# Last batch of a four-layer graph network: adj's transpose and layers 2 and 3 in buffers of layer 0, layer 3 by halves, and a new set of order constants

## The chip, the cores and the metric

The kernel runs on one core of one Trainium2 chip. The metric is the device time of one execution in microseconds (us), the median of the runs shown. Engines are named as in the profile: PE is TensorE (matmul), PEld its weight loads, DVE is VectorE, ACT is ScalarE, POOL is GpSimd, SP is SyncE, which here only issues DMAs.

## The reference

32 graphs ("batches") of 512 nodes with 128 features each, and a 0/1 adjacency matrix per graph with about 16 ones per row. Four layers follow one another, each on the normalised and rectified nodes, each added to `x`:

```
h = relu(layernorm(x)); x = x + max_j( relu(p_i + q_j + b) * adj[i, j] )          # layer 0
h = relu(layernorm(x)); x = x + four tanh layers of: (adj/|row|) @ (f ws), f wn,
                            (adj/|col|).T @ (f wd), each with wu                     # layer 1
h = relu(layernorm(x)); x = x + (adj / rowsum) @ (h w) + bias                       # layer 2
h = relu(layernorm(x)); 4 times:                                                    # layer 3
    m = adj.T @ (h weight[l])
    r, z = sigmoid(m w_ih + h w_hh + b);  n = tanh(m w_ih_n + b_n + r * (h w_hh_n + c_n))
    h = (1 - z) * n + z * h
x = x + h * mask
```

The batches don't depend on each other. Within one batch everything from layer 1 on is one chain: sublayer after sublayer.

## The kernel before, in words

Nodes lie in four tiles of 128 (`NT = 4`), so a batch's node features are one 128 x 512 tile. `an` is the adjacency matrix of a batch in SBUF, `at` its transpose, made on PE and moved out by ACT. Layer 0 (functions `prepare` and `gathers`) finds each node's largest neighbours in two ways at once: 28 indirect DMAs per batch on POOL's queue gather rows of a table (`G`, `gm`, with DVE maxima), and for the rest one-hot matrices (`oh`, made on DVE from `ccd`) pick rows by matmul into `pa`, with DVE maxima into `acc`. Layer 1 is `layer1`, layers 2 and 3 are `layer23`. A float32 operand of an aggregation is split in a high and a low part (`hi`, `lo`), so an aggregation is eight matmuls `pg`.

In layer 3, one sublayer goes: transposes `ph` of the new `h` (PE), `hi` (ACT), `lo` (DVE), aggregation `pg` (PE), `mT` (ACT), the two gates `pk` (PE: a part with `h`, early, and a part with `mT`), two sigmoids (ACT), `phn` and `pxn` (PE), `nn` (DVE twice, then tanh on ACT), then `z*h` on POOL and the new `h` by two DVE instructions. Each handles the whole 128 x 512 tile.

The order of every engine's instructions is fixed when the program is built. A small list scheduler (class `Flow`) holds the operations of up to `AHEAD = 6` batches, keeps a model clock for every engine, and gives out next what can start first; of those that can start at the same time it takes the one with the earliest due time. The due time is `place * PACE - (longest way to the batch's end) - lead`: `place` is the batch's number moved by `LAST`, the lead comes from the table `LEADS`, by stage. A larger lead therefore means: earlier in the queue. `WEIGHTS` are the places of three pieces of weight preparation that are ordered the same way. Where PE would be idle by the model for over 1 us, matmuls without use (`spin`) are put in, so that the granted clock stays up.

Buffers set the rest of the order. A tag (`hi2`, `mT`, `at`, ...) is a ring of so many buffers, handed out strictly in the order of the batches; an operation that writes a buffer for the first time waits until the tile that held it has been read for the last time. Layers 2 and 3 own one buffer each of `xn2`, `hi2`, `lo2`, `mT`, `hg` (the state `h`), `gate0`, `gate1`, `zc`, `nn`; layer 1 has its own ones. `at` and `an` have three each, `af` (the adjacency matrix as loaded) one, `ccd` six. The eight PSUM banks are shared: the four groups `ps0` (layer 0's preparation), `ps1` (layer 1), `ps2` (layers 2 and 3) and `ps3` (layer 0's `pa`) keep 2, 1, 2 and 1, and two are lent to whoever asks.

Of the kernel before, what the change touches and what calls it, by code (L numbers as in the profile page):

```python
# [13 lines left out]
F32 = mybir.dt.float32  # L14
F32R = mybir.dt.float32r
# [3 lines left out]
AF = mybir.ActivationFunctionType  # L19
ALU = mybir.AluOpType  # L20
# [4 lines left out]
P = 128  # L25
# [6 lines left out]
KEY = float(ROWS)  # L32
CODES = ((0, 1), (P, 1), (2 * P, 2), (4 * P, 4))
NLEFT = 7
PACE = 45.28
SPACING = 1.8
AHEAD = 6
BANKS = (2, 1, 2, 1)

LEADS = {  # L40
    "prepare": -31.3, "counts": -26.1, "keys": -29.9, "rows": -0.7,
    "gather0": 21.0, "gather1": 4.8, "gather2": 6.6, "gather3": -2.7,
    "first": 14.9, "layer1": -15.8, "layer10": -31.7, "layer11": -34.7,
    "layer12": -17.6, "layer13": -49.5, "layer2": 17.3, "layer3": 7.8,
    "layer30": 58.6, "layer31": 78.0, "layer32": 36.2, "layer33": 30.6,
    "out": 18.1,
}
LAST = (0.0, 0.0, -0.31, -0.67, 0.62)
WEIGHTS = (-4.52, -3.22, -3.0)
LN_EPS = 1e-5  # L50
L2_EPS = 1e-12
LOWEST = float(np.finfo(np.float32).min)
# [7 lines left out]
def flat(t):  # L60
    return t.rearrange("p t d -> p (t d)")
# [755 lines left out]
def fast(ctx: ExitStack, tc: tile.TileContext, a: dict, out: bass.AP, bad):  # L817
    nc = tc.nc
    x, adj, nodemask = a["x"], a["adj"], a["nodemask"]
    B, N, D = x.shape  # L820
    assert D == P and N % P == 0
    NT = N // P
# [6 lines left out]
    F = Flow(nc, PACE, AHEAD)  # L829
# [5 lines left out]
    def pst(s, name):  # L835
        return bank(s, [P, NT, P], F32, name)

    big = ctx.enter_context(tc.tile_pool(name="big", bufs=1))
    mid = ctx.enter_context(tc.tile_pool(name="mid", bufs=1))
    W = FastWeights(nc, F, a, const, mid, ps)  # L840
# [6 lines left out]
    for i in range(2):  # L847
        t = dram.tile([ROWS, P], F32, name=f"qtab{i}")
        k = (ROWS - 2 * P) // P
        nc.sync.dma_start(  # L850
            out=t[2 * P :, :].rearrange("(k p) d -> p k d", p=P),
# [10 lines left out]
        F.act.dma_start(out=af, in_=adj[b].rearrange("(t p) j -> p t j", p=P))  # L862
        return xt, af

    def norm(s, xt, tag):

        st = F.tile(small, [P, NT, nc.vector.BN_STATS_DIM], F32, tag=f"st{s}", name=f"st_{tag}", bufs=4)
        mv = F.tile(small, [P, NT, nc.vector.BN_AGGR_DIM], F32, tag=f"mv{s}", name=f"mv_{tag}", bufs=4)
        for t in range(NT):
            F.vec.bn_stats(st[:, t, :], xt[:, t, :])  # L870
        for t in range(NT):
            F.vec.bn_aggr(mv[:, t, :], st[:, t, :])
        rstd = F.tile(small, [P, NT], F32, tag=f"rstd{s}", name=f"rstd_{tag}", bufs=4)
        F.vec.tensor_scalar(rstd, mv[:, :, 1], LN_EPS, None, ALU.add)
        F.pool.tensor_tensor(rstd, rstd, W.mhalf[:, 0:NT], ALU.pow)
        shift = F.tile(small, [P, NT], F32, tag=f"shift{s}", name=f"shift_{tag}", bufs=4)
        F.vec.tensor_scalar(shift, mv[:, :, 0], -1.0, None, ALU.mult)
        F.pool.tensor_mul(shift, shift, rstd)
        xn = F.tile(mid, [P, NT, P], F32, tag=f"xn{s}", name=f"xn_{tag}")
        for t in range(NT):  # L880
            F.act.activation(
                xn[:, t, :], xt[:, t, :], AF.Relu,
                bias=shift[:, t : t + 1], scale=rstd[:, t : t + 1],
            )
        return xn

    def transposed(s, src, name):

        pt = pst(s, name)
        for t in range(NT):  # L890
            F.tr(pt[:, t, :], src[:, t, :], W.ident)
        return pt

    def sbuf_parts(s, src, tag):

        hi = F.tile(mid, [P, NT, P], F32R, tag=f"hi{s}", name=f"hi_{tag}")
        F.act.copy(hi, src)
        lo = F.tile(mid, [P, NT, P], F32R, tag=f"lo{s}", name=f"lo_{tag}")
        F.pool.tensor_sub(lo, src, hi.bitcast(F32))
        return hi, lo  # L900

    def parts(s, src, tag):

        hi = F.tile(mid, [P, NT, P], F32R, tag=f"hi{s}", name=f"hi_{tag}")
        F.act.copy(hi, src)
        lo = F.tile(mid, [P, NT, P], F32R, tag=f"lo{s}", name=f"lo_{tag}")
        F.vec.tensor_sub(lo, src, hi.bitcast(F32))
        return hi, lo

    def aggregate(s, two, m, name):  # L910

        pg = pst(s, name)
        hi, lo = two
        for jt in range(NT):
            F.mm(flat(pg), hi[:, jt, :], m[:, jt, :], start=(jt == 0), stop=False)
            F.mm(flat(pg), lo[:, jt, :], m[:, jt, :], start=False, stop=(jt == NT - 1))
        return pg


    def prepare(b, xt, af):  # L920

        deg = F.tile(small, [P, 2, NT], F32, tag="deg", name=f"deg_{b}", bufs=4)
        xn = norm(0, xt, f"{b}_0")
# [10 lines left out]
        pt = transposed(0, xn, f"pt_{b}_0")  # L934
        hT = F.tile(mid, [P, NT, P], F32, tag="hT0", name=f"hT_{b}_0")
        F.act.copy(hT, pt)
        at = F.tile(big, [P, NT, N], F32R, tag="at", name=f"at_{b}", bufs=3)
        for half in range(NT // 2):
            pt = bank(0, [P, 2, N], BF16, f"pat_{b}_{half}")
            for u in range(2):  # L940
                jt = 2 * half + u
# [9 lines left out]
        qn = F.tile(mid, [P, NT, P], F32, tag="qn", name=f"qn_{b}")  # L951
# [34 lines left out]
        ccd = []  # L986
# [161 lines left out]


    def layer23(b, x2, an, at, dinv):  # L1150
        xn = norm(2, x2, f"{b}_2")
        two = sbuf_parts(2, xn, f"{b}_2")
        F.pool.tensor_add(x2, x2, W.b2.unsqueeze(1).to_broadcast([P, NT, P]))
        pg = aggregate(2, two, at, f"pg2_{b}")
        mT = F.tile(mid, [P, NT, P], F32, tag="mT", name=f"mT2_{b}")
        F.act.copy(mT, pg)
        po = pst(2, f"po_{b}")
        for t in range(NT):
            F.mm(po[:, t, :], mT[:, t, :], W.w2, start=True, stop=True)
        x3 = x2  # L1160
        F.lead = LEADS["layer3"]
        for t in range(NT):
            F.vec.scalar_tensor_tensor(
                x3[:, t, :], po[:, t, :], dinv[:, t : t + 1], x2[:, t, :], ALU.mult, ALU.add
            )
        xn = norm(2, x3, f"{b}_3")
        two = sbuf_parts(2, xn, f"{b}_3")
        pt = transposed(2, xn, f"pt_{b}_3")
        h = F.tile(mid, [P, NT, P], F32, tag="hg", name=f"h_{b}_3")
        F.act.copy(h, pt)  # L1170
        for l in range(W.NL3):
            F.lead = LEADS[f"layer3{l}"]
            gates = []
            for k in range(2):
                pk = pst(2, f"pk_{b}_{l}_{k}")
                F.mm(flat(pk), W.gh[l][:, k, :], flat(h), start=True, stop=False)
                gates.append(pk)
            pg = aggregate(2, two, an, f"pg3_{b}_{l}")
            mT = F.tile(mid, [P, N], F32, tag="mT", name=f"mT_{b}_{l}")
            F.act.copy(mT, flat(pg))  # L1180
            for k in range(2):
                F.mm(flat(gates[k]), W.gm[l][:, k, :], mT, start=False, stop=True)
                g = F.tile(mid, [P, N], F32, tag=f"gate{k}", name=f"gate{k}_{b}_{l}")
                c = 3 * l + k
                F.act.activation(g, flat(gates[k]), AF.Sigmoid, bias=W.bsum[:, c : c + 1])
                if k == 1:

                    zc = F.tile(mid, [P, N], F32, tag="zc", name=f"zc_{b}_{l}")
                    F.pool.tensor_scalar(zc, g, -1.0, 1.0, ALU.mult, ALU.add)
                gates[k] = g  # L1190
            r, z = gates
            c = 3 * l + 2
            phn = pst(2, f"phn_{b}_{l}")
            F.mm(flat(phn), W.gh[l][:, 2, :], flat(h), start=True, stop=True)
            nn = F.tile(mid, [P, N], F32, tag="nn", name=f"nn_{b}_{l}")
            F.vec.scalar_tensor_tensor(
                nn, flat(phn), W.bhh[:, c : c + 1], r, ALU.add, ALU.mult
            )
            pxn = pst(2, f"pxn_{b}_{l}")
            F.mm(flat(pxn), W.gm[l][:, 2, :], mT, start=True, stop=True)  # L1200
            F.vec.tensor_add(nn, flat(pxn), nn)
            F.act.activation(nn, nn, AF.Tanh, bias=W.bih[:, c : c + 1])

            F.pool.tensor_mul(z, flat(h), z)
            hn = F.tile(mid, [P, NT, P], F32, tag="hg", name=f"h_{b}_{l}")
            F.vec.tensor_mul(nn, nn, zc)
            F.vec.tensor_add(flat(hn), z, nn)
            h = hn
            pt = transposed(2, h, f"ph_{b}_{l}")
            if l + 1 < W.NL3:  # L1210
                two = parts(2, pt, f"{b}_3_{l}")
        F.lead = LEADS["out"]
        xo = F.tile(mid, [P, NT, D], F32, tag="mT", name=f"xo_{b}")
        for t in range(NT):
            c = b * NT + t
            F.vec.scalar_tensor_tensor(
                xo[:, t, :], pt[:, t, :], W.mcol[:, c : c + 1], x3[:, t, :], ALU.mult, ALU.add
            )
        F.act.dma_start(out=out[b].rearrange("(t p) d -> p t d", p=P), in_=xo)
# [15 lines left out]

    F.spin = spin

    places = [b - LAST[max(0, b - B + len(LAST) - 1)] for b in range(B)]
    F.run(
        list(zip(WEIGHTS, (W.first, W.rest, W.last)))  # L1240
        + [(p, partial(batch, b)) for b, p in enumerate(places)]
# [471 lines left out]
```

## Time and profile before

| | |
|---|---|
| median of 3 runs | 2977.16 us (2974.79 to 2977.79) |
| the profiled execution, device time | 2976.68 us |
| its span, first to last instruction | 2975.0 us |
| PE busy | 2861.7 us, of which 69.7 us are `spin` |
| DVE, POOL, ACT busy | 2393.3, 1819.8, 1216.1 us |
| PE clock granted | 0.990 of full speed on average |
| one batch in the middle of the run | 87 us |

The profile comes from one execution, and the times in it are microseconds from the first instruction. All compute instructions are issued from a few helper lines, so groups are told apart by the names of their tiles (out<-in), not by lines. A busy PE isn't a PE at work on the result: the `spin` matmuls count as busy.

### The profile page before, as it was taken

Reading aid. Unit: us, or ns where it says so; the run is one execution under the profiler, and the core shown is the slowest. Engines: PE = TensorE matmul, PEld = TensorE weight load, DVE = VectorE, ACT = ScalarE, POOL = GpSimd, SP = SyncE. Lnnn points to the kernel's source line nnn. Section 1 sums busy time; section 2 is a strip of 40 time slices with the busy share of each in tenths; the row PEclk is TensorE's granted clock in tenths of the full one; section 3 lists DMA queues with packets and bytes.
Section 4 is the critical chain, followed back from the end, with each engine's and each line's share of the span. In section 5 each row is a group of like instructions: output and inputs, shape, how many; then the busy total and the mean of one; then the engine's idle time right before and its main releaser. Section 6 shows DMA issues by size and latency. Waiting matters only on the chain.

```text
span 2975.0 us, 37664 instructions
## 1 busy us (share of the span) xinstructions
PE 2861.7 (96%) x11490; PEld 1752.8 (59%) x11490; DVE 2393.3 (80%) x5363; ACT 1216.1 (41%) x2528; POOL 1819.8 (61%) x2005
## 2 busy tenths in 40 slices
PE   7789999999999999999999999999999999999997
PEld 4455556666666666666666666666666666655553
DVE  6978878988888898888889888888988888887532
ACT  3333434434444443444444344444434444433322
POOL 3666766666666666666666666666666666654411
PEclk9989999999999999999999999999999999999999
DMA  7553334334334333333443333344333334321200
GB/s 171 109 94 71 63 76 86 82 74 83 62 65 85 86 78 77 75 65 69 86 86 78 78 74 65 70 85 86 77 79 74 64 72 85 67 54 43 33 4 5
DMA packets 191266, 218.43 MB, mean 73 GB/s; under 512 B 30376, under 2 KB 139600, under 8 KB 191056
## 3 DMA queue, kind: packets, MB, share of 16 engines
q0 software_dynamic: 47104, 92.34, 22.5%
q1 hardware_dynamic: 73768, 63.63, 7.3%
q10 hardware_dynamic: 70184, 59.98, 6.5%
q8 instruction: 93, 1.52, 0.2%
q14 instruction: 117, 0.96, 0.1%
HBM read 164.32 MB, written 17.96 MB: 61 GB/s over the span
## 4 chain that ended last, share of the span: by engine, by line
PE 78%; DVE 12%; issue 4%; DMA 2%; ACT 2%; POOL 2%; DVEq 0%; SPq 0%; ACTq 0%; POOLq 0%
PE pg L504 23%; PE pu L504 18%; PE pk L504 15%; PE pa L504 6%; PE pxn L504 4%; PE phn L504 4%; DVE acc L504 3%; PE pkey L504 2%; PE ph L504 2%; PE pf L504 1%; DVE nn L504 1%; DVE qhl L504 1%; PE pt L504 1%; DVE oh L504 1%; DVE x L504 1%
## 5 line engine op out<-in xcount | busy, mean ns | idle before, releaser
L504 POOL DMA_INDIRECT G<-qtab,idx x768 | 840.8, 1095 | 574.5 <-DVE gm L504 461.5
L504 DVE TENSOR_TENSOR acc<-acc,pa 128x512 f32<-128x512 f32 x992 | 673.6, 679 | 146.3 <-PE pa L504 134.2
L504 PE MATMUL pa<-oh,qhl 128*128 128x512 f32 x1024 | 472.1, 512 | 10.8 <-DVE acc L504 6.6
L504 PE MATMUL pg<-an,hi 128*128 128x512 f32 x1024 | 458.8, 448 | 2.0 <-DVE lo L504 1.6
L504 PE MATMUL pu<-ag,w 128*128 128x512 f32 x896 | 449.3, 595 | 1.5 <-DVE ag L504 1.3
L504 PE MATMUL pg<-an,lo 128*128 128x512 f32 x1024 | 432.8, 424 | 0.0
L504 DVE TENSOR_SCALAR oh<-ccd 128x1024 fp32r<-128x1024 bf16 x512 | 392.2, 783 | 13.6 <-PE pa L504 12.6
L504 PE MATMUL pg<-at,lo 128*128 128x512 f32 x640 | 296.7, 464 | 0.6 <-POOL lo L504 0.5
L504 PE MATMUL pg<-at,hi 128*128 128x512 f32 x640 | 287.7, 449 | 6.9 <-ACT hi L504 3.2
L504 PEld LDWEIGHTS pa<-oh,qhl 128*128 128x128 f32 x1024 | 194.2, 191 | 143.9 <-issue 43.6
L504 DVE TENSOR_TENSOR gm<-gm,G 128x128 f32<-128x128 f32 x768 | 258.6, 338 | 5.5 <-DMA G<-qtab,idx 4.6
L504 PE MATMUL pk<-h,g_hh 128*128 128x512 f32 x512 | 258.4, 608 | 1.8 <-ACT h L504 1.1
L504 ACT ACTIVATE xn<-x,shift,rstd 128x128 f32<-128x128 f32 x512 | 211.6, 484 | 107.5 <-POOL shift L504 107.5
L504 PEld LDWEIGHTS pg<-an,hi 128*128 128x128 f32 x1024 | 192.7, 188 | 97.0 <-issue 49.0
L504 PEld LDWEIGHTS pg<-an,lo 128*128 128x128 f32 x1024 | 193.0, 188 | 85.9 <-issue 42.0
L504 PE MATMUL pk<-mT,g_ih 128*128 128x512 f32 x512 | 241.7, 594 | 1.1 <-ACT mT L504 1.1
L504 PEld LDWEIGHTS pu<-ag,w 128*128 128x128 f32 x896 | 169.5, 190 | 118.1 <-issue 82.8
L504 ACT ACTIVATE gate<-pk,bsum 128x512 f32<-128x512 f32 x256 | 175.7, 686 | 147.8 <-PE pk L504 144.5
L504 POOL TENSOR_TENSOR rstd<-rstd,mhalf 128x4 f32<-128x4 f32 x128 | 144.1, 1126 | 138.0 <-DVE shift L504 135.9
L504 ACT COPY mT<-pg 128x512 f32<-128x512 f32 x160 | 93.7, 586 | 328.3 <-PE pg L504 324.0
L504 DVE TENSOR_TENSOR ag<-pg,rbc 128x512 f32<-128x512 f32 x256 | 174.5, 683 | 42.8 <-PE pg L504 39.7
L504 ACT CAST hi<-ph 128x512 fp32r<-128x512 f32 x96 | 56.3, 586 | 365.2 <-PE ph L504 362.2
(169 smaller groups left out, 5135.2 us busy)
## 6 DMA issues: line engine op xcount, KB each, us to landing
af<-in_adj_dram ACTq DMA_DIRECT2D x32, 1024.0 KB
ccd<-cc SPq DMA_DIRECT2D x512, 64.0 KB
an<-in_adj_dram POOLq DMA_DIRECT2D x128, 256.0 KB, 3.7
x<-in_x_dram ACTq DMA_DIRECT2D x64, 256.0 KB
rbc<-scal SPq DMA_DIRECT2D x32, 512.0 KB
G<-qtab,idx POOLq DMA_INDIRECT x768, 3.8
qtab<-qn SPq DMA_DIRECT2D x128, 64.0 KB
out_dram<-xo ACTq DMA_DIRECT2D x32, 256.0 KB
```

Source lines behind the costliest of these rows:

```text
L504: op.fn(*(real(v) for v in op.args), **{k: real(v) for k, v in op.kw.items()})
```

## The change

Four things, and a new set of numbers.

- The last batch's `at` goes into the buffer of `af`, which no later load needs, and so no longer waits for a buffer of the ring `at`.
- In the last batch, layers 2 and 3 take their SBUF tiles from rings of layer 0 (table `LATE`: `xn0`, `qn`, `gm`, `acc`, `hT0`, `pn`, `ccd`) and their PSUM banks from `ps0`, so they no longer wait for the batch ahead to leave the buffers of layers 2 and 3.
- In the last batch, layer 3 runs by two halves of the nodes, 256 columns each: every instruction of a sublayer but the four transposes is issued once per half. The aggregation of a half still needs all of `h`.
- Both gates of a half share one PSUM bank, as do `phn` and `pxn` of a half.
- `LEADS`, `LAST`, `WEIGHTS` and `PACE` have new values, and a new table `FIRST` moves the places of the first four batches. These hold for all batches.

For all other batches the instructions stay the same; the two gates' matmuls with `mT` are now both noted ahead of the two sigmoids.

```diff
-PACE = 45.28
+PACE = 45.35
 LEADS = {
-    "prepare": -31.3, "counts": -26.1, "keys": -29.9, "rows": -0.7,
-    "gather0": 21.0, "gather1": 4.8, "gather2": 6.6, "gather3": -2.7,
-    "first": 14.9, "layer1": -15.8, "layer10": -31.7, "layer11": -34.7,
-    "layer12": -17.6, "layer13": -49.5, "layer2": 17.3, "layer3": 7.8,
-    "layer30": 58.6, "layer31": 78.0, "layer32": 36.2, "layer33": 30.6,
-    "out": 18.1,
+    "prepare": -33.2, "counts": -28.6, "keys": -38.2, "rows": -9.6,
+    "gather0": 12.6, "gather1": -3.5, "gather2": -1.7, "gather3": -10.5,
+    "first": 14.4, "layer1": -15.5, "layer10": -39.2, "layer11": -39.2,
+    "layer12": -26.1, "layer13": -57.9, "layer2": 50.7, "layer3": 187.5,
+    "layer30": 155.2, "layer31": 193.8, "layer32": 81.5, "layer33": 66.2,
+    "out": 33.8,
 }
-LAST = (0.0, 0.0, -0.31, -0.67, 0.62)
-WEIGHTS = (-4.52, -3.22, -3.0)
+FIRST = (-0.01, -0.0, -0.31, 0.0)
+LAST = (0.0, -0.23, -0.17, -0.97, -0.05)
+WEIGHTS = (-5.87, -1.69, -2.33)
+LATE = {
+    "xn2": ("xn0", 1), "hi2": ("qn", 1), "lo2": ("gm", 1), "mT": ("acc", 1), "hg": ("hT0", 1),
+    "gate0": ("pn", 2), "gate1": ("ccd", 6), "zc": ("ccd", 6), "nn": ("ccd", 6),
+}
...
-        at = F.tile(big, [P, NT, N], F32R, tag="at", name=f"at_{b}", bufs=3)
+        home = ("af", 1) if b == B - 1 else ("at", 3)
+        at = F.tile(big, [P, NT, N], F32R, tag=home[0], name=f"at_{b}", bufs=home[1])
...
     def layer23(b, x2, an, at, dinv):
-        xn = norm(2, x2, f"{b}_2")
-        two = sbuf_parts(2, xn, f"{b}_2")
+        own = dict(LATE) if b == B - 1 else {}
+        s = 0 if own else 2
+        def buf(dtype, tag, name):
+            tag, bufs = own.get(tag, (tag, 1))
+            pool = big if tag == "ccd" else mid
+            return F.tile(pool, [P, NT, P], dtype, tag=tag, name=name, bufs=bufs)
+        xn = norm(2, x2, f"{b}_2", buf)
+        two = sbuf_parts(2, xn, f"{b}_2", buf)
...
+        step = NT // 2 if own else NT
+        cuts = [slice(t, t + step) for t in range(0, NT, step)]
...
-            pg = aggregate(2, two, an, f"pg3_{b}_{l}")
-            mT = F.tile(mid, [P, N], F32, tag="mT", name=f"mT_{b}_{l}")
-            F.act.copy(mT, flat(pg))
+            mT = buf(F32, "mT", f"mT_{b}_{l}")
+            for c in cuts:
+                pg = pst(s, f"pg3_{b}_{l}_{c.start}")
+                pg = pg if step == NT else pg[:, 0:step, :]
+                hi, lo = two
+                for jt in range(NT):
+                    m = an[:, jt, c.start * P : c.stop * P]
+                    F.mm(flat(pg), hi[:, jt, :], m, start=(jt == 0), stop=False)
+                    F.mm(flat(pg), lo[:, jt, :], m, start=False, stop=(jt == NT - 1))
+                F.act.copy(cut(mT, c), pg)
...
+            for c, (vh, vx) in zip(cuts, halves):
+                F.mm(flat(vh), W.gh[l][:, 2, :], flat(cut(h, c)), start=True, stop=True)
+                F.vec.scalar_tensor_tensor(
+                    cut(nn, c), vh, W.bhh[:, n : n + 1], cut(r, c), ALU.add, ALU.mult
+                )
+                F.mm(flat(vx), W.gm[l][:, 2, :], flat(cut(mT, c)), start=True, stop=True)
+                F.vec.tensor_add(cut(nn, c), vx, cut(nn, c))
+                F.act.activation(
+                    cut(nn, c), cut(nn, c), AF.Tanh, bias=W.bih[:, n : n + 1]
+                )
+                F.pool.tensor_mul(cut(z, c), cut(h, c), cut(z, c))
+                F.vec.tensor_mul(cut(nn, c), cut(nn, c), cut(zc, c))
+                F.vec.tensor_add(cut(hn, c), cut(z, c), cut(nn, c))
+                for t in range(c.start, c.stop):
+                    F.tr(pt[:, t, :], hn[:, t, :], W.ident)
...
-    places = [b - LAST[max(0, b - B + len(LAST) - 1)] for b in range(B)]
+    places = [
+        b - FIRST[min(b, len(FIRST) - 1)] - LAST[max(0, b - B + len(LAST) - 1)] for b in range(B)
+    ]
```

## The prediction

> **What bounds the kernel now.** I read the page's first two parts, then the stretches of PE with the `spin` matmuls apart, then the waits of PE, then the timeline of the end.
>
> ```profile
> PE 2861.7 (96%) x11490; PEld 1752.8 (59%) x11490; DVE 2393.3 (80%) x5363; ACT 1216.1 (41%) x2528; POOL 1819.8 (61%) x2005
> PE   7789999999999999999999999999999999999997
> 500.00:2500.00 2000.00, 1970.71 (x7986) 1.00 0.38 77
> 2700.00:2800.00 100.00, 95.81 (x351) 1.00 0.28 43
> 2800.00:2894.00 94.00, 91.28 (x314) 1.00 0.03 9
> 2894.00:2963.00 69.00, 59.16 (x214) 0.98 0.01 4
> 2894.00:2963.00 69.00, 22.89 (x96) 0.98 0.01 4
> PE ph L504 <- DVE h L504: 18.9, 31, 1.0
> PE po L504 <- DVE x L504: 15.3, 30, 0.5
> ```
>
> PE is the bound. A line of a stretch gives start and end, its length, PE's busy time and instructions, the granted clock, DMA share and GB/s; the second line for 2894 to 2963 is of `spin` alone. Useful PE work is 2861.7 - 69.7 = 2792.0 us, so 2975.0 - 2792.0 = 183 us of the span are lost on PE. By stretch, busy less `spin`: 91 us before 500; 29 us in the 2000 us of the middle (1.5%); about 5 from 2500 to 2700; 100 - 95.8 + 2.4 = 6.6 from 2700 to 2800; 94 - 91.3 + 4.4 = 7.1 up to 2894; 69 - (59.2 - 22.9) = 33 up to 2963; 12 in the last transfer and the closing flag. The two waits are those of the middle: about 1.1 us per batch, where PE reaches `ph` and `po` before DVE is through.
>
> The 33 us are the case of this change. What stands there, one sublayer of layer 3 of the last batch, `spin` and repeats left out:
>
> ```profile
> 2944.39 1.98 PE L504 MATMUL pk<-mT,g_ih 128*128 128x512 f32 x4 [0.28 <-ACT mT L504]
> 2945.55 0.69 ACT L504 ACTIVATE gate<-pk,bsum 128x512 f32<-128x512 f32 x1 [1.22 <-PE pk L504]
> 2946.28 0.75 DVE L504 SCALAR_TENSOR_TENSOR nn<-phn,bcol,gate 128x512 f32<-128x512 f32 x1 [5.63 <-ACT gate L504]
> 2947.27 0.69 DVE L504 TENSOR_TENSOR nn<-pxn,nn 128x512 f32<-128x512 f32 x1 [0.24 <-PE pxn L504]
> 2947.99 0.72 ACT L504 ACTIVATE nn<-nn,bcol 128x512 f32<-128x512 f32 x1 [0.89 <-DVE nn L504]
> 2948.82 0.89 DVE L504 TENSOR_TENSOR nn<-nn,zc 128x512 f32<-128x512 f32 x1 [0.86 <-ACT nn L504]
> 2949.81 0.69 DVE L504 TENSOR_TENSOR h<-gate,nn 128x512 f32<-128x512 f32 x1
> 2950.65 0.63 PE L504 MATMUL ph<-ident,h 128*128 128x128 f32 x4 [0.83 <-DVE h L504]
> 2951.37 0.59 ACT L504 CAST hi<-ph 128x512 fp32r<-128x512 f32 x1 [2.65 <-PE ph L504]
> 2951.99 0.69 DVE L504 TENSOR_TENSOR lo<-ph,hi 128x512 fp32r<-128x512 f32 x1 [1.48 <-ACT hi L504]
> 2956.42 1.98 PE L504 MATMUL pk<-mT,g_ih 128*128 128x512 f32 x4 [0.28 <-ACT mT L504]
> ```
>
> From `pk` at 2944.39 to `pk` at 2956.42 a sublayer takes 12.0 us, a pure chain. PE's useful part of it is six gate products at 0.86, eight `pg` at 0.23 and the transposes 0.45: 7.4 us. The batch ahead ended at 2893.68 (its last `ph`), just when layer 1 of the last batch did (`px` at 2893.19), so nothing is left to fill the gaps.
>
> **What the Trainium skill says.** "VectorE: DVE Perf Modes", section "The TRN2 errata": VectorE and ScalarE pay a fixed cost per instruction; its formula for a float32 two-tensor operation, (N+151)/0.96 ns, gives 691 ns for 512 columns (the trace: 0.69) and 424 for 256 (the trace's 128x256 additions: 416 to 419 ns). Its ScalarE row from PSUM, 172 + columns at 1.2 GHz, gives 570 and 357 ns (the trace: 586 for 512). "TensorE: Matmul & The Clock Gate", section "LDWEIGHTS": 128 weight columns take 107 ns, an estimate for the half products, whose streaming of 256 columns takes as long; the trace shows 188 to 190 ns for the `pg` loads, hidden behind 230 ns matmuls. Same page, Part 1: PE falls to half clock after an idle window; the trace agrees, with `pg` every 0.43 us at 2903 instead of 0.23. "SBUF — State Buffer", section "SBUF: two separate sides": DVE with two SBUF inputs and POOL exclude each other; the product with `zc` takes 0.89 while POOL multiplies, 0.69 elsewhere.
>
> **The change, part by part.**
>
> *Halves.* On the chain of a sublayer stand, at full width, `hi`, `lo`, `mT`, one sigmoid, four DVE steps and a tanh. At 256 columns each gets shorter by 0.21 (ACT: 256/1.2) or 0.27 (DVE: 256/0.96): four ACT steps and five DVE steps, 4 x 0.21 + 5 x 0.27 = 2.2 us. The PE products before the first sigmoid, `pxn` and the transposes of the second half save some 0.9 more. Against that the second half follows the first one by about one instruction (0.5 to 0.7 us), and one `hg` buffer is left, so the first half of the new `h` can't be written before POOL has multiplied the second half's `z`: another 0.5. Net 12.0 - 2.2 - 0.9 + 1.1 = 10.0, a gain of 2.0 us. Bounds: if the 16 half `pg` go at 0.19 (the loads) instead of 0.11, 16 x 0.08 = 1.3 of it goes, leaving 0.7; if the lag hides fully, 3.1. I take 2.0 for each of four sublayers: 8 us, from 3 to 12.
>
> *Own buffers for layers 2 and 3 of the last batch.* Its layer 2 no longer waits for `hi2`, `lo2`, `xn2` of the batch ahead. In this trace that wait was short, as both ended at 2893. What goes: four `xo` of the batch ahead on DVE (1.12) ahead of the statistics, POOL's `x<-x,b` (1.27) ahead of `lo`, and the half clock in layer 2 (8 x 0.2 = 1.6): 2 to 4 us, I take 3. More comes only if layer 1 of the last batch ends earlier than layer 3 of the batch ahead.
>
> *`at` in the buffer of `af`.* Now the transpose of the last batch is moved out at 2660, behind layer 2 of the batch three ahead, its last counts come at 2719, its gathers run from 2732 to 2792, `x1` is written at 2807 and its layer 1 starts at 2810. With the buffer free the transposes can go some 90 us earlier (its `ab` is there by 2555); the gathers then wait for `gm`, which the batch ahead leaves at 2682, so `x1` can come up to 50 us earlier. That isn't 50 us of time: layer 1 of the batch ahead ends at 2815 (its last `f`) and holds layer 1's buffers. It moves some 15 us of PE work and the DVE maxima out of the end, and takes a second condition away. No DMA is added; `af` is wanted by no later load. I count 4 us, of the 13.7 lost from 2700 to 2894.
>
> *The new constants.* Layer 3's lead over layer 1's first sublayer rises from 58.6 + 31.7 = 90 us to 155.2 + 39.2 = 194. Batch 30 moves back by 0.30 places (14 us), batch 31 by 0.67 (30 us). So layer 3 goes first wherever both are ready, and layer 1 fills its gaps. For the last two batches this means: layer 1 of batch 31 gives way to layer 3 of batch 30, which keeps the two side by side as now and leaves layers 2 and 3 of batch 31 alone at the end. In the middle both directions are open: at best the 34.2 us of `ph` and `po` waits go; at worst layer 3, issued as soon as the model clock lets it, makes PE wait at 12 hand-overs per batch (`ph`, `pg`, `pk` of four sublayers). With 0.1 us at each that is 1.2 us x 28 batches = 34 us. DVE at 80% and the queue order behind it decide. The lower-priority work of layers 0 and 1 is a larger reserve for PE, which speaks for a small gain: I take 5 us for middle and start together, with ±34 as bounds. `WEIGHTS` and `FIRST` move weight preparation behind the first batch's layer 0; PE is idle there anyway (40 us of the first 74), so nothing is counted.
>
> Sum: 8 + 3 + 4 + 5 = 20 us. The profiled execution took 2976.68 (span 2975.0 plus 1.7 around it), 0.5 under the median: 2977.2 - 20 = 2957.
>
> **Rivals.**
>
> *A, the forecast: the tail gets shorter by some 15 us, the middle a little better.* 2957, own range 2946 to 2968. For it: chain and gaps are in the trace.
>
> *B, batches 30 and 31 side by side in layer 3.* If layer 1 of the last batch is through before layer 3 of batch 30, two chains with 7.4 us of PE each fill 12 us, and of the 33 us lost only some 8 remain; with half of the 13.7: 25 + 7 + 5 = 37 less, 2940. For it: own buffers and banks make it possible. Against it: layer 3's larger lead.
>
> *C, the tail gains less and the middle gives it back.* If half products are bound by weight loads and own buffers find nothing to overlap, 3 + 2 from the tail and nothing from the order: 2972.
>
> *D, slower: layer 3 without slack.* With the lead of 194 us the scheduler places layer 3's matmuls at the moment the model has them ready. PE issues in order, so a DVE result that comes 0.1 to 0.2 us late at `ph`, `pg` or `pk` stalls everything behind it, layer 1 included. The tail's 15 us are used up from 15/28 = 0.54 us per batch on; at 1.1 us per batch: 31 - 15 = 16 later, 2993. For it: `ph` already waits for `h` in 31 batches. Against it: each such wait is now only 0.6 us, and more work lies ready.
>
> That the change doesn't reach the last batch at all can be left out: nothing else claims the rings in `LATE` at that time.
>
> **How the numbers follow.** A 0.44, B 0.18, C 0.20, D 0.18. The prediction is A's time, 2957. A measurement of this kernel can tell 0.2% (6 us) from no change. A and B are faster; C lies across the line, half of it (0.10) faster and half the same; D is slower. Faster 0.72, same 0.10, slower 0.18. The range has to hold A and C, most of B and half of D: 2934 to 2993, with about 0.08 below and 0.10 above. A's own range is 2946 to 2968.
>
> **What would show it.** Halves: the step from `pk` to `pk` in the last batch's layer 3 near 10 us; near 11.3 with `pg` 0.19 apart if weight loads bind. Own buffers: layer 2's `pg` of the last batch before the last `ph` of batch 30, in B by tens of us. `at`: the last transposes' evictions near 2570 instead of 2660, the last gathers ended by about 2750. Order: the period in the middle 86.8 or less instead of 87; in D 88, with PE waits on `h`, `hi`, `lo` and `mT` in each batch. The forecast is wrong if the middle moves by over 15 us either way, which no row of this trace excludes.

## The result, and the profile after

| | before | after |
|---|---|---|
| median | 2977.15 us (2974.79 to 2977.79) | 2940.44 us (2936.14 to 2943.54) |
| profiled execution, its span | 2976.68, 2975.0 us | 2943.54, 2941.8 us |
| PE busy, of it `spin` | 2861.7, 69.7 us | 2843.4, 54.0 us |
| one batch in the middle | 86.97 us | 86.57 us |

The ratio is 0.9877, with an interval of 0.986 to 0.9894: 36.7 us faster. That is the time of rival B (2940), not of the likeliest case (2957, own range 2946 to 2968). A profile shows one execution, and here it is the slowest of the changed kernel's four, so the spans of the two profiles differ by 33.2 us only. The period is the distance of two outputs: their DMAs are issued at 1519.63 and 1606.60 before, at 1510.03 and 1596.60 after. Over the 16 batches from 1086 to 2476 before and from 1078 to 2463 after it is 86.87 and 86.60 us.

The first part of the page after the change:

```profile
PE 2843.4 (97%) x11493; PEld 1753.8 (60%) x11513; DVE 2384.2 (81%) x5382; ACT 1218.1 (41%) x2547; POOL 1827.3 (62%) x2013
```

PE in the middle after the change, and PE from 2700 to the end: before, all of it and then `spin` alone, and after, all and `spin` alone (columns as in the prediction):

```profile
500.00:2500.00 2000.00, 1979.22 (x7999) 1.00 0.37 77
2700.00:2975.00 275.00, 246.91 (x879) 0.98 0.12 21
2700.00:2975.00 275.00, 29.68 (x119) 0.98 0.12 21
2700.00:2941.80 241.80, 219.38 (x829) 0.98 0.09 19
2700.00:2941.80 241.80, 13.13 (x47) 0.98 0.09 19
```

PE's loss is the length of a stretch less what PE is busy, plus `spin`, the same sum as in the prediction. Before 500 it is 89.8 us instead of 91.3; in the middle (500 to 2500) 20.8 instead of 29.3; from 2700 to the end 35.6 instead of 57.8, of which 11 are the last transfer and the flag. So the end gave 22 us, the middle 8.5, the start 1.5; from 2500 to 2700 the loss rose by 1.6, and the useful PE time fell by 2.6, which makes up the 33.2.

The waits of PE that the prediction named, over the whole run after the change, and then `ph` between 500 and 2500, before and after (us in total, times, longest):

```profile
PE po L510 <- DVE x L510: 16.0, 31, 1.0
PE ph L510 <- DVE h L510: 7.3, 11, 1.4
PE ph L504 <- DVE h L504: 12.7, 21, 0.6
PE ph L510 <- DVE h L510: 0.8, 2, 0.4
```

In the middle, `ph` hardly waits for `h` any more. `po` waits for `x` as before.

The end, in the timeline before the change: `x1` of the last batch (`x` with layer 0 added, written by POOL), the last tanh of layer 1 of batch 30 (`f`), the end of layer 1 of the last batch (`px`), and the last transposes of batch 30 (`ph`).

```profile
2807.18 1.29 POOL L504 TENSOR_TENSOR x<-gm,x 128x512 f32<-128x512 f32 x1 [1.45 <-issue]
2815.42 0.69 ACT L504 ACTIVATE f<-pu,bu 128x512 f32<-128x512 f32 x1
2893.19 0.66 PE L504 MATMUL px<-ident,f 128*128 128x128 f32 x4 [0.35 <-ACT f L504]
2893.68 0.60 PE L504 MATMUL ph<-ident,h 128*128 128x128 f32 x4
```

After the change: the same three of `x1`, `f` and `px`, the start of the last batch's layer 2 (`pg`), five transposes, three of them batch 30's (its fourth and last is at 2898.87), and then the first transposes of two sublayers of the last batch by halves.

```profile
2773.36 1.27 POOL L510 TENSOR_TENSOR x<-gm,x 128x512 f32<-128x512 f32 x1 [1.44 <-issue]
2785.22 0.69 ACT L510 ACTIVATE f<-pu,bu 128x512 f32<-128x512 f32 x1 [0.27 <-PE pu L510]
2862.82 0.66 PE L510 MATMUL px<-ident,f 128*128 128x128 f32 x4 [0.35 <-ACT f L510]
2871.36 0.80 PE L510 MATMUL pg<-at,hi 128*128 128x512 f32 x1
2897.46 0.71 PE L510 MATMUL ph<-ident,h 128*128 128x128 f32 x5
2907.24 0.44 PE L510 MATMUL ph<-ident,h 128*128 128x128 f32 x2 [0.36 <-DVE h L510]
2917.91 0.41 PE L510 MATMUL ph<-ident,h 128*128 128x128 f32 x2 [1.09 <-DVE h L510]
```

Before, `px` came half a microsecond ahead of the last `ph` of batch 30. Now it comes 36 us ahead of that, and layer 2 and the first sublayer of the last batch run in the gaps of batch 30's layer 3. `x1` comes 34 us earlier, and layer 1 of batch 30 ends at 2785 instead of 2815. `x1` is there 7 us ahead of that before and 11 us after, and in both kernels the last batch's own layer 1 ends 77 us behind it (its last tanh is at 2892.45 before and 2862.08 after). The last transposes of the last batch's `at` are moved out by 2606 instead of 2662. A sublayer by halves takes 10.7 and 11.2 us where it is alone (first transposes at 2907.24, 2917.91, 2929.12).

### The profile page after: what moved, and what is told of

It reads as the page before. It is cut to its first block, busy times and chain, and to the rows that moved or that the text cites. A ratio compares the mean times of both kernels' runs of the same rounds, so it can differ in the third digit from the quotient of the medians.

```text
span 2941.8 us, 37748 instructions
## 1 busy us (share of the span) xinstructions
PE 2843.4 (97%) x11493; PEld 1753.8 (60%) x11513; DVE 2384.2 (81%) x5382; ACT 1218.1 (41%) x2547; POOL 1827.3 (62%) x2013
## 4 chain that ended last, share of the span: by engine, by line
PE 80%; DVE 10%; issue 4%; DMA 2%; ACT 2%; POOL 1%; ACTq 0%; SPq 0%; DVEq 0%; POOLq 0%
PE pg L510 25%; PE pu L510 19%; PE pk L510 15%; PE pa L510 6%; PE phn L510 4%; PE pxn L510 3%; DVE acc L510 3%; PE pkey L510 2%; PE ph L510 2%; PE pf L510 2%; PE po L510 1%; DMA G<-qtab,idx 1%; DVE nn L510 1%; PE pt L510 1%; DVE x L510 1%
## 5 line engine op out<-in xcount | busy, mean ns | idle before, releaser
L510 PE MATMUL pa<-oh,qhl 128*128 128x512 f32 x1024 | 465.7, 510 | 11.2 <-DVE oh L510 5.3
L510 PE MATMUL pg<-an,hi 128*128 128x512 f32 (+1 forms) x1040 | 457.3, 441 | 0.6 <-DVE acc L510 0.4
L510 PE MATMUL pg<-an,lo 128*128 128x512 f32 (+1 forms) x1040 | 436.0, 422 | 0.0
L510 PE MATMUL pg<-at,hi 128*128 128x512 f32 x640 | 281.1, 439 | 7.2 <-DVE acc L510 1.8
L510 PE MATMUL pk<-h,g_hh 128*128 128x512 f32 (+1 forms) x528 | 256.3, 590 | 0.6 <-DVE top L510 0.6
L510 PE MATMUL pk<-mT,g_ih 128*128 128x512 f32 (+1 forms) x528 | 242.3, 580 | 1.4 <-ACT mT L510 1.1
L510 ACT ACTIVATE gate<-pk,bsum 128x512 f32<-128x512 f32 (+1 forms) x264 | 176.9, 673 | 140.8 <-PE pk L510 137.3
L510 ACT COPY mT<-pg 128x512 f32<-128x512 f32 (+1 forms) x164 | 94.2, 575 | 304.6 <-PE pg L510 300.0
L510 ACT CAST hi<-ph 128x512 fp32r<-128x512 f32 (+1 forms) x99 | 56.8, 574 | 341.2 <-PE ph L510 333.4
```

Source lines behind the costliest of these rows:

```text
L510: op.fn(*(real(v) for v in op.args), **{k: real(v) for k, v in op.kw.items()})
```

## The experiments

Each is timed against the kernel before, whose median was 2977 to 2980 us in these sessions. "Middle" and "end" are the losses of PE in us, from 500 to 2500 and from 2700 on, from the one execution of each that was profiled; it lies up to 7 us off the median. Useful PE time itself differs between these orders (2786 to 2810 us by the records), so a difference in time isn't the difference of losses to the microsecond. The new numbers came with the whole change, so an experiment that takes a part out can show two things at once: what the part is worth, and what the order loses where the numbers no longer fit it.

| kernel | median us | ratio to before (interval) | middle | end |
|---|---|---|---|---|
| before | 2977 to 2980 | 1 | 29.3 | 57.8 |
| the change | 2940.44 | 0.9877 (0.986 to 0.9894) | 20.8 | 35.6 |
| numbers alone | 2969.06 | 0.9968 (0.9954 to 0.9982) | 18.5 | 58.2 |
| `at` and numbers | 2963.35 | 0.9944 (0.9928 to 0.9961) | 19.6 | 57.1 |
| `at` alone, old numbers | 2980.44 | 1.0002 (0.9993 to 1.0011) | 28.4 | 58.6 |
| all but the numbers | 2965.25 | 0.996 (0.9946 to 0.9974) | 28.9 | 47.7 |
| all but the halves | 2950.32 | 0.9902 (0.9886 to 0.9919) | 20.0 | 42.7 |
| all but own buffers | 2955.25 | 0.9921 (0.9905 to 0.9938) | 20.4 | 52.1 |
| all but `at` | 2979.08 | 1.0004 (0.9995 to 1.0013) | 20.8 | 59.2 |
| old leads of layers 2 and 3 | 2965.58 | 0.9957 (0.9945 to 0.997) | 25.0 | 38.5 |
| old `LAST` | 2945.32 | 0.9899 (0.9882 to 0.9915) | 19.6 | 36.1 |
| old `WEIGHTS`, no `FIRST` | 3011.1 | 1.0113 (1.0096 to 1.013) | 62.9 | 36.7 |
| old `WEIGHTS` | 3021.4 | 1.0136 (1.0119 to 1.0153) | 73.8 | 36.7 |
| `po` as a whole | 3003.13 | 1.0086 (1.007 to 1.0103) | 50.4 | 39.5 |

**The numbers alone.** The kernel before with the new values of `LEADS`, `FIRST`, `LAST`, `WEIGHTS`, `PACE` and the new line for `places`; of its diff against before:

```diff
-PACE = 45.28
+PACE = 45.35
...
-LAST = (0.0, 0.0, -0.31, -0.67, 0.62)
-WEIGHTS = (-4.52, -3.22, -3.0)
+FIRST = (-0.01, -0.0, -0.31, 0.0)
+LAST = (0.0, -0.23, -0.17, -0.97, -0.05)
+WEIGHTS = (-5.87, -1.69, -2.33)
```

> The kernel before with only the new LEADS, FIRST, LAST, WEIGHTS and PACE; at in its ring, layers 2 and 3 of the last batch in the shared buffers and whole. Theory S (the last batch's layer 1 gets ahead, so that its layers 2 and 3 stand beside layer 3 of batch 30; that needs own buffers and the new order together): the middle keeps its 8 us, the tail gains nothing, 2967 to 2972. Theory F (the forecast's sum, each part by itself: halves 8, own buffers 3, at 4, numbers 5): 2972. Theory N (the new numbers do it all): 2945 or less.

As S has it: the middle gains 11 us, the end nothing (58.2). N falls; F's 2972 lies inside the interval too, so F isn't excluded by this run.

**All but the numbers.** `LEADS` is that of before, too.

```diff
-PACE = 45.35
+PACE = 45.28
...
-FIRST = (-0.01, -0.0, -0.31, 0.0)
-LAST = (0.0, -0.23, -0.17, -0.97, -0.05)
-WEIGHTS = (-5.87, -1.69, -2.33)
+LAST = (0.0, 0.0, -0.31, -0.67, 0.62)
+WEIGHTS = (-4.52, -3.22, -3.0)
+FIRST = (0.0,)
```

> The changed kernel with LEADS, LAST, WEIGHTS and PACE of before and no FIRST: own buffers, at in af's buffer and halves alone. S: some of the overlap appears, since buffers no longer forbid it, but the order doesn't ask for it: 2955 to 2968. F: 2977 - 15 = 2962. N: 2972 to 2977.

2965.25 is inside S and three away from F; it doesn't tell these two apart. The middle stays at 28.9 with the old waits of `ph` (12.3 us): the middle is the numbers' work. The end gains 10 of 22 us. Here the last batch's `x1` comes at 2789 and its layer 1 ends at 2884; with the new numbers 2773 and 2862.

**All but the halves.**

```diff
-        step = NT // 2 if own else NT
+        step = NT
```

> The changed kernel with layer 3 of the last batch whole (step = NT), own buffers, at and numbers kept. S: in the trace of the changed kernel a sublayer by halves takes 10.7 to 11.2 us instead of 12.0 and two of four stand beside other work, so the halves are worth 2 to 4 us: 2943 to 2945. F: 8 us, 2948. N: 2940.

The end loses 42.7 instead of 35.6, so the halves are worth 7 us there (10 by the medians), near F's 8 and more than S said. Where a sublayer is alone it takes 12.1 us (first transposes at 2914.19, 2926.31, 2938.39). By the timelines the last transposes start 9.3 us later than in the changed kernel; 2.9 of that are there already at `px` (2865.70), ahead of the first instruction by halves. The remaining 6.4 split evenly: 3.2 up to the first sublayer's transposes, 3.1 in the three sublayers behind them.

**All but own buffers.**

```diff
-        own = dict(LATE) if b == B - 1 else {}
-        s = 0 if own else 2
+        own = {}
+        s = 2
...
-        step = NT // 2 if own else NT
+        step = NT // 2 if b == B - 1 else NT
```

> The changed kernel with layers 2 and 3 of the last batch back in the buffers and banks of layers 2 and 3 (no LATE, PSUM group ps2), halves, at and numbers kept. S: layer 2 of the last batch has to wait for the last aggregation of batch 30 again, its start moves from 2871 to about 2898 and the end by 20 to 27 us: 2960 to 2967. F: 3 us, 2943. N: 2940.

The median lies between F and S and much nearer to S: 14.8 us by the medians instead of 3, and 16.5 us of loss at the end in the profiled execution, which is the slowest of its four (2961.89). In its timeline, the end of layer 1 of the last batch, the last transposes of batch 30 and the first product of the last batch's layer 2:

```profile
2862.78 0.66 PE L510 MATMUL px<-ident,f 128*128 128x128 f32 x4 [0.35 <-ACT f L510]
2887.60 0.63 PE L510 MATMUL ph<-ident,h 128*128 128x128 f32 x4 [1.10 <-DVE h L510]
2887.98 0.48 PE L510 MATMUL pg<-at,hi 128*128 128x512 f32 x1
```

Layer 1 is through at 2862.8 as in the changed kernel, and layer 2 then stands until batch 30 has left the buffers.

**All but `at`.**

```diff
-        home = ("af", 1) if b == B - 1 else ("at", 3)
+        home = ("at", 3)
```

> The changed kernel with the last batch's at back in the ring of three (own buffers, halves, numbers kept). Theory S2 (the early at takes layer 0 of the last batch out of the time in which layer 1 of batch 30 runs, so that layer 1 of batches 30 and 31 ends about 20 to 30 us earlier): the last evictions of at move from 2603 back to about 2650, x1 of the last batch from 2773 to about 2787 or later, layer 1 of batch 31 ends near 2880 instead of 2862, time 2953 to 2961. Theory F (4 us for at): 2944.

Both theories fall short: nothing is left of the gain, though the middle keeps its 8.5 us. Its timeline at the end:

```profile
2807.56 1.27 POOL L510 TENSOR_TENSOR x<-gm,x 128x512 f32<-128x512 f32 x1 [1.44 <-issue]
2893.26 0.65 PE L510 MATMUL px<-ident,f 128*128 128x128 f32 x4 [0.41 <-ACT f L510]
```

`x1` is back at 2807.6, and layer 1 of the last batch ends 7 us after batch 30's last transposes (2886.1), so own buffers have nothing to overlap. But not all of this is the wait for a buffer of the ring: the kernel with the numbers alone has `at` in the ring as well, and yet its `x1` comes at 2786.9 and it is 10 us faster. In both, `at` is moved out by 2656. The two orders part at the last batch's key products `pkey`: the last of them run at 2721 here and at 2700 there, and so the last gathers start at 2730 and at 2706. Why the scheduler put these products back was not tried.

**`at` with the numbers, and `at` alone.** The kernel before with the lines of `home` and, in the first of the two, the new numbers.

```diff
-        at = F.tile(big, [P, NT, N], F32R, tag="at", name=f"at_{b}", bufs=3)
+        home = ("af", 1) if b == B - 1 else ("at", 3)
+        at = F.tile(big, [P, NT, N], F32R, tag=home[0], name=f"at_{b}", bufs=home[1])
```

> The kernel before with the new numbers and at of the last batch in af's buffer; layers 2 and 3 of the last batch in the shared buffers and whole. Theory S2 (at is what brings layer 1 of the last batch forward): x1 of the last batch near 2773 and the end of its layer 1 near 2862 as in the changed kernel, then layer 2 waits for batch 30 until about 2890 and the sublayers take 12.0: 2958 to 2964. Theory J (at pays only together with own buffers): 2967 to 2971, as the new numbers alone.

> The kernel before with at of the last batch in af's buffer and nothing else. S2: with the old order the last evictions of at come near 2612 and layer 1 of the last batch ends near 2884 instead of 2893, as with all three parts under the old numbers: 2966 to 2971. J: 2975 to 2979.

S2 holds for the first in time and place: `x1` at 2772.0, the last tanh of layer 1 at 2862.5, and then the wait for batch 30, whose last transposes are at 2888.1; layer 2's `po` follows at 2893.8. J holds for the second, whose time is 1.4 us above J's range; S2's place for layer 1 is met there too, its time is not. In its timeline stand the end of layer 1 of the last batch, the last transposes of batch 30, and layer 2's first product:

```profile
2884.96 0.66 PE L504 MATMUL px<-ident,f 128*128 128x128 f32 x4 [0.35 <-ACT f L504]
2898.33 0.63 PE L504 MATMUL ph<-ident,h 128*128 128x128 f32 x4 [1.25 <-DVE h L504]
2898.71 0.48 PE L504 MATMUL pg<-at,hi 128*128 128x512 f32 x1
```

Layer 1 is through 13 us ahead of batch 30, and layer 2 starts only behind it. So two conditions stand one behind the other: the end of the last batch's layer 1, and the buffers of layers 2 and 3. Under the new numbers, with neither part the end loses 58.2, with `at` alone 57.1, with own buffers and halves alone 59.2, with `at` and own buffers 42.7. (By the medians `at` alone is 5.7 us faster than neither part.)

**The larger lead of layer 3.**

```diff
-    "layer12": -26.1, "layer13": -57.9, "layer2": 50.7, "layer3": 187.5,
-    "layer30": 155.2, "layer31": 193.8, "layer32": 81.5, "layer33": 66.2,
+    "layer12": -26.1, "layer13": -57.9, "layer2": 17.3, "layer3": 7.8,
+    "layer30": 58.6, "layer31": 78.0, "layer32": 36.2, "layer33": 30.6,
```

> The changed kernel with the leads of layer2, layer3 and layer30 to layer33 of before, all else new. Theory L (the larger lead of layer 3 is what takes away PE's waits for h in the middle): the waits of ph for h between 500 and 2500 come back to about 12 us, the loss there rises from 20 to about 28, time 2949 or more. Theory M (the other new numbers do that): the middle stays at 20, time 2938 to 2945.

The time is on L's side, its reason isn't: the waits of `ph` don't return (0.6 us). The period is 87.47 us (outputs at 1517.26 and 1604.73), worse than either kernel's, which is some 20 us over the middle; only 4.2 of them show as loss (25.0), while the useful PE time by the records is 11.8 us longer over the whole run. What makes the period longer stays open. The end is nearly as good as with the large lead, 38.5.

**Old `LAST`.**

```diff
-LAST = (0.0, -0.23, -0.17, -0.97, -0.05)
+LAST = (0.0, 0.0, -0.31, -0.67, 0.62)
```

> The changed kernel with LAST of before: batch 31 at place 30.38 and batch 30 at 30.67 instead of 31.05 and 30.97. If it is buffers and the lead of layer 3 that set the tail, the places hardly matter: 2936 to 2946. If batch 30 had to be put back so that its layer 3 stays beside that of batch 31: layer 1 of batch 31 ends later or layer 3 of batch 30 earlier, tail loss up from 36 to 45, 2950. The middle doesn't change in either case.

The end loses 36.1 and layer 1 of the last batch ends at 2862 as in the changed kernel: the places of the last batches hardly matter. The median is 4.9 us above the changed kernel's, with overlapping intervals. The places that the expectation names are one entry off: by the line for `places`, batches 28 to 31 take the first four entries of `LAST`, and the fifth is never used. So the old places are 29.00, 30.31 and 31.67 for batches 29 to 31, the new ones 29.23, 30.17 and 31.97.

**Old start.** `WEIGHTS` of before with no `FIRST`, as in the diff, and then `WEIGHTS` alone.

```diff
-FIRST = (-0.01, -0.0, -0.31, 0.0)
+FIRST = (0.0,)
...
-WEIGHTS = (-5.87, -1.69, -2.33)
+WEIGHTS = (-4.52, -3.22, -3.0)
```

> The changed kernel with WEIGHTS of before and no FIRST. The start lost 91.3 us of PE before the change and 89.8 after it, so the two should be worth nothing by themselves: 2936 to 2946, with about 90 lost before 500. If the start was a gain hidden by another loss: 2950 or more.

> The changed kernel with WEIGHTS of before, FIRST kept. WEIGHTS and FIRST of before together cost 70 us. If it is WEIGHTS (the weights of layers 1 and 3 made too early or too late for the new leads of layer 0): 3000 to 3015, the loss from 297 to 1000 near 60. If it is FIRST (the third batch's place): 2936 to 2946.

It is `WEIGHTS`: 80 us. The start itself shows little of it, 94.0 lost before 500 against 89.8. In the stretch that follows, for old `WEIGHTS`, every engine (PE, PEld, DVE, ACT, POOL, each with its instructions):

```profile
300.00:1000.00 700.00, 666.20 (x2639) 404.95 (x2646) 544.38 (x1241) 282.43 (x589) 425.29 (x464) 0.98 0.35 70
1500.00:2500.00 1000.00, 987.97 (x4005) 615.15 (x4004) 848.12 (x1918) 435.07 (x905) 655.90 (x719) 1.00 0.37 77
```

All engines do less from 300 to 1000, with 13.5 us of PE's being `spin`, and from 1500 on the kernel runs as usual. Its outputs come at distances of 80 to 125 us until about 1330, while the changed kernel has its 87 us from about 560 on. The order falls into its period late; which operation holds it back was not tried.

**`po` as a whole.**

```diff
-            F.mm(po[:, t, :], mT[:, t, :], W.w2, start=True, stop=True)
+            F.mm(po[:, t, :], mT[:, t, :], W.w2, start=True, stop=True, group=po)
```

> The changed kernel with the four products po of layer 2 taken as writers of the whole tile, so that DVE's first read of po comes behind the fourth product instead of the third. Theory W (the wait of po for x, 0.5 us in 23 of 23 batches of the middle in every kernel so far, is the fourth product waiting for DVE's read of the same bank, made by the order of issue and not by a late DVE): the wait goes, the loss in the middle falls from 20.8 to about 10, 12 to 16 us in all: 2925 to 2930. Theory V (PE waits as long elsewhere): 2937 to 2944.

The wait is gone. PE's waits from 1500 to 2500 of this kernel, all that the view lists:

```profile
PE pu L510 <- ACT rows L510: 1.9, 2, 1.2
PE ph L510 <- DVE h L510: 0.3, 1, 0.3
```

Between 1500 and 2500 it loses 4.8 us where the changed kernel loses 10.2, and batches come 85.7 to 86.6 us apart. But it too falls into its period late, with 101.5 us lost before 500 and 37.7 from 500 to 1000, and is slower than before as a whole. W is right about the wait and wrong about the time, and V's time isn't met either. With new numbers fitted to it, half a microsecond per batch might be won, which was not tried.

## Why the prediction was right, and where it was wrong

The direction, the two places (end and middle) and the range held. The size did not: 36.7 us instead of 20, outside the likeliest case's own range, because parts that open a way for one another were priced one by one.

*`at`, 4 us.* The step that failed: "That isn't 50 us of time: layer 1 of the batch ahead ends at 2815". That `x1` comes earlier was right (34 us, with `at` out by 2606; forecast: up to 50, and near 2570), and the last batch's layer 1 does follow batch 30's, 77 us from end to end in both kernels. But 2815 wasn't a fixed time. Layer 1 of batch 30 ends 95 us behind that of batch 29 in the kernel before, 84 with the new numbers alone, 85 with everything but `at`, and 72 with everything. That it no longer shares its time with layer 0 of the last batch is the likely reason, by the timelines only. Taken out of the change, this part costs all of the 36 us; some of that is the order, which then also puts the last `pkey` back, so the worth of `at` by itself isn't shown.

*Own buffers, 3 us.* The step said that more comes only if layer 1 of the last batch ends earlier than layer 3 of batch 30. It does, by 36 us, and the term is 15 us by the medians. The condition was named, its price was put into rival B.

*Halves, 8 us.* Near in size: 6.4 us at the end by the timelines. The step from 12.0 to 10.0 was too good, 10.7 to 11.2. The half products `pg` go every 0.12 us, so weight loads don't bind. The term that was too small is the wait for POOL, put at 0.5. In the sublayer of 10.7 us:

```profile
2915.82 0.42 DVE L510 TENSOR_TENSOR nn<-nn,zc 128x256 f32<-128x256 f32 x1
2916.58 0.73 POOL L510 TENSOR_TENSOR gate<-h,gate 128x256 f32<-128x256 f32 x1
2917.34 0.42 DVE L510 TENSOR_TENSOR h<-gate,nn 128x256 f32<-128x256 f32 x1 [0.77 <-POOL gate L510]
```

The first half's product with `zc` is through at 2916.24, and the first half of the new `h` starts 1.1 us later, when POOL's second product is through. In the sublayer ahead of it DVE's products also meet POOL's:

```profile
2904.97 1.59 POOL L510 TENSOR_TENSOR gate<-h,gate 128x256 f32<-128x256 f32 x2
2905.05 1.80 DVE L510 TENSOR_TENSOR nn<-nn,zc 128x256 f32<-128x256 f32 x2
```

Two half products of DVE take 1.80 us there, and 1.30 in the sublayer of 11.2 us, against 0.42 each in the one of 10.7, which agrees with the exclusion that the Trainium skill describes ("SBUF — State Buffer", "SBUF: two separate sides").

*The new numbers, 5 us.* They gave 8.5 in the middle, by `ph` as the better bound had it. Which of the values takes the waits of `ph` away stays open: with the old leads of layers 2 and 3 they don't return. That bound, 34.2 us, counts the waits of the whole run; between 500 and 2500 they are 24.5, and `po`'s 11.8 of them could not go. The step read `po` as a late DVE. It is the fourth product waiting until DVE has read the first quarter of the same tile, put there by the order of issue; it stood in every order looked at but the one that took it away. The places of the last batches were read one entry off, too: batch 31 moves back by 0.30 places and batch 30 forward by 0.14, not back by 0.67 and 0.30. By the run with the old `LAST` this changes little.

*B, whose time was met.* Its mechanism is there: layer 2 of the last batch starts 27 us ahead of the end of batch 30. Its sum is met in part by luck: it had 32 us from the end and 5 from the middle and the start, and the profiles show 22 and 10. What it held against itself, "layer 3's larger lead", didn't weigh. With the old lead the end loses 38.5, with the new one 35.6. What had kept the two batches apart was the late layer 1 of batch 30 and the shared buffers.

*`WEIGHTS`, nothing.* PE is idle in the start, as said, but the start decides when the period is reached: the old values with the new leads cost 80 us. Rival D did not come: no new waits of PE on `h`, `hi`, `lo` or `mT` in the middle. Rival C is excluded by the 22 us at the end.

## What to carry to other kernels

Where two conditions gate the same start, an edit alone may show little or nothing, and look like one to drop: price them together, and ask of each time that is called fixed what else ran in front of it. In an order that a scheduler computes, constants fit one program: any later edit, even one that removes a real wait, has to be judged with constants fitted again, by its settled part apart from its start.

## What was not expected of the hardware

A stream of products with 256 columns, each with a weight load of its own, ran at 0.12 us per product (the `pg` of the last batch from 2920.7 to 2922.3), though each of these loads is shown with 0.19 us. So the length that the profile shows for a load isn't the time by which it holds up the stream.
